# Products with Wu in column tiles of 32, four in turn over two tiles; the halo rows of the automaton network held for two rows of blocks at a time

## The chip, the cores and the metric

The kernel runs on one core of a Trainium2 chip. The metric is device time in microseconds (us), the median of repeated executions. A trace shows one profiled execution: its span runs from the first to the last instruction. The engines named below are TensorE (PE; its weight loads are listed apart as PEld), VectorE (DVE), ScalarE (ACT), GpSimd (POOL) and SyncE (SP), which here only issues DMA transfers.

## The reference: what is computed

The input x is 32 images of 8 channels, 256 x 256, float32. Four layers follow, each `x = x + layer(groupnorm(x))`. Only layer 0 is touched by the change:

```python
drive = x[:, :C_OUT]
grid = drive
for _ in range(15):                       # a coupled-map automaton
    mapped = R * grid * (1.0 - grid)
    local = conv3x3_per_channel(mapped, K_local)
    physics = (1.0 - EPS) * mapped + EPS * local
    grid = (1.0 - BETA) * physics + BETA * drive
cml_out = clip(grid, 0.0001, 1.0 - 0.0001)
h = relu(conv3x3(x, Wp, bp))              # 8 -> 128 channels
nca_out = sigmoid(conv1x1(h, Wu, bu))     # 128 -> 8 channels
gin = concat([x, cml_out, nca_out])       # 24 channels
g = sigmoid(conv1x1(relu(conv3x3(gin, Wg1, bg1)), Wg2, bg2))
layer0 = g * cml_out + (1.0 - g) * nca_out
```

Layers 1 to 3 are 3x3 and 5x5 convolutions of 8 channels. The product with Wu has 128 inputs and only 8 outputs for a pixel.

## The kernel before

There are two phases. The first (lines 148 to 450) computes layer 0 of all images and stores them in DRAM; the second (from line 453) computes layers 1 to 3. The change lies in the first.

An image of 256 rows is seen as 16 blocks (k) of 16 rows (r). Two streams of work are written as generators and interleaved by the loop at line 442.

`lattice(b)` is the automaton for image b. It loads and normalizes the image, transposes it into patches, and makes 15 steps. A step treats the eight channels in two halves of four. For each channel TensorE makes two products, one with the patches themselves (line 278) and one with a ring of neighbours (line 279), both float32 and 512 columns wide; DVE makes two operations on the result (lines 286 and 288); and after each half four DMA transfers on SP copy the new neighbours to `rings` (`spread`, line 210). The next step's ring products of that half wait for these transfers.

`gated(b)` is the rest of layer 0 for the image before, whose data the automaton has finished. It runs over eight values of r2, and each covers two blocks k = 2 r2 and 2 r2 + 1, in all their rows: 16 values of r, 2 x 256 pixels each.

- `hidden(r2)` brings nine-fold shifted input to `im` (6 transfers on ACT's queue for each half of eight rows). For each row r it makes the product with Wp (line 359: 72 inputs, 128 outputs, 512 columns) to a PSUM tile `ph`, applies ReLU on ACT into `hh` (line 364), and multiplies `hh` with Wu (line 343). This product is issued one row late. Its result has 8 useful rows, and it is to land on partitions 8 r to 8 r + 7 of one PSUM tile `psn`; so the stationary matrix is a window of 128 columns in a wide zero matrix `wu_sb`, in which Wu stands at column 8 r, and the 16 products accumulate. Then ACT takes the sigmoid into `nh` (line 370), and two transfers on SP copy the rows which neighbouring row groups need from `nh` to `hb` (`beside`, line 312).
- `gate(r2)` is run after `hidden(r2 + 1)`, since it needs the halo of the blocks below. It makes nine products for the three sources and three column shifts (line 392), one with the halo `ha` of x and the automaton (line 397, called the wga product), one with `hb` (line 398, the wgb product), ReLU, the product with Wg2 (line 403), sigmoid, and the mix on POOL and DVE.

The order of instructions on each engine is made by a scheduler when the program is built: it takes the traced instructions by priority, which follows the order of the text, and lets later ones pass those that it holds not to be ready. [...] The PSUM tiles of `ph`, `pg`, `pq` and the transposes share three buffers; `hh`, `g1` and `gt` share three buffers in SBUF.

Of the kernel before, what the change touches and what calls it, by code (L numbers as in the profile page):

```python
# [9 lines left out]
F32 = mybir.dt.float32  # L10
# [8 lines left out]
C = 8  # L19
# [41 lines left out]
def kernel(  # L61
# [10 lines left out]
    def const(pool, src, shape, name):  # L72
        t = pool.tile(shape, F32, name=name)
        nc.sync.dma_start(t, src)
        return t
# [72 lines left out]
    with ExitStack() as es:  # L148
# [13 lines left out]
        wu_sb = const(wt, wu, [P, 2 * P - C], "wu_sb")  # L162
# [23 lines left out]
        nh = wt.tile([P, HB, WP], F32, name="nh")  # L186
        ha = wt.tile([96, HB, WP], F32, name="ha")
        hb = wt.tile([72, HB, WP], F32, name="hb")
        state = wt.tile([P, C, SN], F32, name="state")
        rings = [wt.tile([RING, 4, SN], F32, name=f"rings{i}") for i in range(2)]  # L190
        for t in (xb, nh, ha, hb, state, *rings):
            nc.gpsimd.memset(t, 0.0)
# [119 lines left out]
        def beside(queue, t, src, q, blocks):  # L312

            k0, n = blocks
            for i, (p, to) in enumerate(((P - C, k0 + 1), (0, k0 - 1))):
                skip, last = max(0, -to), max(0, to + n - HB)
                m = n - skip - last
                row = HB * WP
                long = m * WP - 2
                queue.dma_start(  # L320
                    t[q + 24 * i : q + 24 * i + 24, :, :].rearrange("p k w -> p (k w)")[
                        :, (to + skip) * WP : (to + skip) * WP + long
                    ],
                    window(src, p * row + (k0 + skip) * WP, [[row, C], [1, 3], [1, long]]),
                )

        def gated(b):

            xn, xr, nr, cr = xn_d[b % 2], xr_d[b % 2], nr_d[b % 2], cr_d[b % 2]
            beside(nc.gpsimd, ha, nr, 0, (0, HB))
            beside(nc.gpsimd, ha, cr, 48, (0, HB))
# [4 lines left out]
            def hidden(r2):  # L338
                pn = ps_n.tile([P, 512], F32, name="psn")
                late = None  # L340

                def second(hh, r):
                    nc.tensor.matmul(  # L343
                        pn, wu_sb[:, C * (RB - 1 - r) : C * (RB - 1 - r) + P], hh,
                        start=r == 0, stop=r == RB - 1,
                    )

                for half in range(2):
                    im = imp.tile([72, 2, 8 * WP], F32, name="im")
                    for dy in range(3):  # L350
                        for k in range(2):
                            at = ((2 * r2 + k) * RB + 8 * half + dy) * WP
                            nc.scalar.dma_start(
                                im[24 * dy : 24 * dy + 24, k, 0:run],
                                window(xn, at, [[HP * WP, C], [1, 3], [1, run]]),
                            )
                    for j in range(8):
                        ph = psum.tile([P, 512], F32, name="ph", tag="ps")
                        nc.tensor.matmul(  # L359
                            ph.rearrange("p (k w) -> p k w", w=W), wp_sb,  # L360
                            im[:, :, j * WP : j * WP + W], start=True, stop=True,
                        )
                        hh = hp.tile([P, 512], F32, name="hh")
                        nc.scalar.activation(hh, ph, AF.Relu, bias=bp_sb)  # L364
                        if late is not None:
                            second(*late)
                        late = (hh, 8 * half + j)
                        yield
                second(*late)
                nc.scalar.activation(  # L370
                    nh[:, 2 * r2 : 2 * r2 + 2, 1 : 1 + W],
                    pn.rearrange("p (k w) -> p k w", w=W), AF.Sigmoid, bias=bu_sb,
                )
                beside(nc.sync, hb, nh, 0, (2 * r2, 2))
# [3 lines left out]
            def gate(r2):  # L378
                k0 = 2 * r2
                if r2 % 2 == 0:  # L380
                    for name, t in (("xq", nr), ("cq", cr)):
                        quarter[name] = qp.tile([P, 4, WP], F32, name=name)
                        nc.scalar.dma_start(quarter[name], t[:, k0 : k0 + 4, :])
# [6 lines left out]
                for s, src in enumerate((xq, cq, nh[:, k0 : k0 + 2, :])):  # L390
                    for dx in range(3):
                        nc.tensor.matmul(  # L392
                            o, wg1_sb[:, s, dx, :], src[:, :, dx : dx + W],
                            start=s == dx == 0, stop=False,
                        )
                    yield
                nc.tensor.matmul(o, wga_sb, ha[:, k0 : k0 + 2, 0:W], start=False, stop=False)  # L397
                nc.tensor.matmul(o, wgb_sb, hb[:, k0 : k0 + 2, 0:W], start=False, stop=True)  # L398
                g1 = hp.tile([P, 512], F32, name="g1", tag="hh")
# [4 lines left out]
                gt = hp.tile([P, 2, W], F32, name="gt", tag="hh")  # L404
                nc.scalar.activation(gt.rearrange("p r w -> p (r w)"), pq, AF.Sigmoid, bias=bg2_sb)  # L405
                ci = cq[:, :, 1 : 1 + W]
                ni = nh[:, k0 : k0 + 2, 1 : 1 + W]
# [185 lines left out]
def laid_out(inputs):  # L593
# [68 lines left out]
    wu = np.zeros((P, 2 * P - C), f)  # L662
    wu[:, P - C : P] = inputs["L0_conv_Wu"][:, :, 0, 0].T
# [15 lines left out]
    for g in range(4):  # L679
# [8 lines left out]
        wu=wu,  # L688
# [43 lines left out]
```

## Time and profile before

| | |
|---|---|
| median of 3 runs | 23432.1 us (23431.12 to 23445.79) |
| profiled execution | 23433.82 us, span 23432.0 us |
| mean granted TensorE clock | 0.962 |
| busy share PE, DVE, ACT, POOL | 94%, 35%, 17%, 5% |
| products with Wp (L359), with Wu (L343) | 8192 records each |
| automaton's products (L278, L279) | 7680 records each |
| last store of the automaton (L308), first | 407.6 us; last one 17906.1 us |

In a row of the profile a name such as `psn<-hh,wu_sb` says what the instruction writes and reads, L343 is a line of the kernel, and xN a count; after the bar stand busy time, mean nanoseconds of one, and the engine's idle time just ahead of these instructions with what ended it. A float32 product shows up as two matmul records and two weight loads.

### The profile page before, as it was taken

The page shows a single profiled execution, that of the slowest core. Times are in us where ns is not written, and L with a number is a line of the kernel's source. Part 1 is how long each engine was busy: PE and PEld are TensorE (multiplying, and loading weights), DVE is VectorE, ACT ScalarE, POOL GpSimd, SP SyncE. Part 2 cuts the span into 40 slices and gives each one's busy share as a digit, 9 for nine tenths or more (in the row PEclk, how much of TensorE's full clock was granted, in tenths as well). Part 3 has the DMA queues.
Part 4 walks back from the last instruction along what each step waited for, and adds up shares of the span by engine and source line. Part 5 has one row for each costly group of instructions (what it writes and reads, how often), then busy time and mean ns, then how long its engine had stood idle before and what let it go on. Part 6 is the DMA issues. An engine that isn't in the chain of part 4 may idle for free.

```text
span 23432.0 us, 148223 instructions
## 1 busy us (share of the span) xinstructions
PE 21942.2 (94%) x52808; PEld 9629.6 (41%) x52808; DVE 8279.5 (35%) x13690; ACT 4064.1 (17%) x5794; POOL 1160.9 (5%) x1071
## 2 busy tenths in 40 slices
PE   7999999999999999999999999999999899999999
PEld 3444444444444444444444444444444344444444
DVE  4333333333333333333333333333332223223222
ACT  0222222222212222221212222122122100000000
POOL 0000000000000000000000000000000000000000
PEclk8999999999999999999999999999999999999999
DMA  5444444444444444444444444444443111111111
GB/s 106 110 111 109 110 109 110 110 112 109 110 110 109 109 111 110 113 107 110 115 110 112 112 110 110 110 109 110 110 111 85 60 58 54 53 52 54 54 50 47
DMA packets 623925, 2269.01 MB, mean 97 GB/s; under 512 B 103160, under 2 KB 302472, under 8 KB 461400
## 3 DMA queue, kind: packets, MB, share of 16 engines
q1 hardware_dynamic: 346200, 997.10, 20.9%
q10 hardware_dynamic: 172032, 810.61, 12.1%
q0 software_dynamic: 104960, 451.82, 6.6%
q8 instruction: 424, 6.95, 0.1%
q14 instruction: 309, 2.53, 0.0%
HBM read 1130.77 MB, written 471.37 MB: 68 GB/s over the span
## 4 chain that ended last, share of the span: by engine, by line
PE 87%; DMA 6%; DVE 5%; ACT 1%; issue 1%; POOL 0%; SPq 0%; ACTq 0%; DVEq 0%; POOLq 0%
PE psn L343 15%; PE ph L359 15%; PE psc L279 13%; PE psc L278 13%; PE psv L496 10%; PE psv L570 9%; PE pg L392 7%; DMA xb<-in_x 2%; DMA cr_d<-xb 1%; PE pq L403 1%; DMA im<-xn_d 1%; PE pg L398 1%; PE pg L397 1%; DMA hb<-nh 1%; DVE bn L234 1%
## 5 line engine op out<-in xcount | busy, mean ns | idle before, releaser
L286 DVE SCALAR_TENSOR_TENSOR state<-psc,dr 128x512 f32<-128x512 f32 x3840 | 2625.5, 689 | 7848.0 <-PE psc L279 6693.4
L359 PE MATMUL ph<-im,wp_sb 72*128 72x512 f32 x8192 | 4201.0, 611 | 115.2 <-DMA hb<-nh 56.1
L343 PE MATMUL psn<-hh,wu_sb 128*128 128x512 f32 x8192 | 4228.0, 608 | 28.5 <-ACT hh L364 28.3
L364 ACT ACTIVATE hh<-ph,bp_sb 128x512 f32<-128x512 f32 x4096 | 2809.5, 687 | 8164.5 <-PE ph L359 6633.6
L278 PE MATMUL psc<-state,patch_sb 128*128 128x512 f32 x7680 | 3919.2, 596 | 105.2 <-DVE state L286 103.4
L279 PE MATMUL psc<-rings,ring_sb 80*128 80x512 f32 x7680 | 3916.5, 594 | 32.4 <-DMA rings<-state 32.4
L288 DVE SCALAR_TENSOR_TENSOR state<-state 128x512 f32<-128x512 f32 x3584 | 2461.7, 706 | 64.4
L359 PEld LDWEIGHTS ph<-im,wp_sb 72*128 72x128 f32 x8192 | 1591.0, 195 | 2145.1 <-issue 1432.2
L343 PEld LDWEIGHTS psn<-hh,wu_sb 128*128 128x128 f32 x8192 | 1532.4, 193 | 2174.0 <-issue 1723.4
L278 PEld LDWEIGHTS psc<-state,patch_sb 128*128 128x128 f32 x7680 | 1449.4, 190 | 2007.4 <-issue 1757.8
L279 PEld LDWEIGHTS psc<-rings,ring_sb 80*128 80x128 f32 x7680 | 1459.9, 190 | 1898.6 <-issue 1880.5
L570 PE MATMUL psv<-xr,w_sb 128*128 128x512 f32 x5120 | 2220.8, 592 | 7.3 <-DVE xr L560 7.3
L496 PE MATMUL psv<-xh,w_sb 128*128 128x512 f32 x4608 | 1987.9, 593 | 23.4 <-ACT xh L128 23.4
L570 PEld LDWEIGHTS psv<-xr,w_sb 128*128 128x128 f32 x5120 | 960.7, 189 | 1201.7 <-issue 1197.2
L496 PEld LDWEIGHTS psv<-xh,w_sb 128*128 128x128 f32 x4608 | 868.4, 189 | 1129.6 <-issue 1093.0
L411 POOL TENSOR_TENSOR gt<-gt,df 128x512 f32<-128x512 f32 x256 | 324.5, 1267 | 14360.0 <-ACT gt L405 14360.0
L400 ACT ACTIVATE g<-pg,bg_sb 128x512 f32<-128x512 f32 x256 | 175.9, 687 | 3924.1 <-PE pg L398 3371.6
L542 DVE SCALAR_TENSOR_TENSOR x<-psv,b_sb,x 128x512 f32<-128x512 f32 x256 | 192.2, 751 | 1676.8 <-PE psv L496 1676.8
L576 DVE TENSOR_TENSOR y<-psv,y 128x512 f32<-128x512 f32 x256 | 176.9, 691 | 1564.8 <-PE psv L570 1564.8
L392 PE MATMUL pg<-cq,wg_sb 128*128 128x512 f32 x1536 | 716.6, 592 | 0.0
L392 PE MATMUL pg<-xq,wg_sb 128*128 128x512 f32 x1536 | 701.8, 592 | 0.0
L392 PE MATMUL pg<-nh,wg_sb 128*128 128x512 f32 x1536 | 700.9, 592 | 0.0
(132 smaller groups left out, 8705.6 us busy)
## 6 DMA issues: line engine op xcount, KB each, us to landing
im<-xn_d ACTq DMA_DIRECT2D x3072, 193.3 KB
rings<-state SPq DMA_DIRECT2D x1920, 213.8 KB
rings<-state SPq DMA_DIRECT2D x1920, 142.5 KB
xn_d<-xb POOLq DMA_DIRECT2D x32, 2064.0 KB, 23.8
nr_d<-xb POOLq DMA_DIRECT2D x32, 2064.0 KB, 33.6
xq<-nr_d ACTq DMA_DIRECT2D x128, 516.0 KB
cr_d<-xb POOLq DMA_DIRECT2D x32, 2064.0 KB, 10.2
cq<-cr_d ACTq DMA_DIRECT2D x128, 516.0 KB
```

Source lines behind the costliest of these rows:

```text
L234: nc.vector.bn_stats(bn[:, r, :], xb[:, r, 1 : 1 + W])
L278: nc.tensor.matmul(o, patch_sb[:, c, :], v, start=True, stop=False)
L279: nc.tensor.matmul(o, ring_sb[:, c, :], rings[half][:, c % 4, 0 : TX * SY].rearrange("p (x y) -> p x y", y=SY)[:, :, 0:TY], start=False, s ...
L286: nc.vector.scalar_tensor_tensor(v, o, FLOOR, dr[:, c], ALU.max, ALU.add)
L288: nc.vector.scalar_tensor_tensor(v, v, 1.0, v, ALU.subtract, ALU.mult)
L343: nc.tensor.matmul(pn, wu_sb[:, C * (RB - 1 - r) : C * (RB - 1 - r) + P], hh, start=r == 0, stop=r == RB - 1,)
L359: nc.tensor.matmul(ph.rearrange("p (k w) -> p k w", w=W), wp_sb, im[:, :, j * WP : j * WP + W], start=True, stop=True,)
L364: nc.scalar.activation(hh, ph, AF.Relu, bias=bp_sb)
L392: nc.tensor.matmul(o, wg1_sb[:, s, dx, :], src[:, :, dx : dx + W], start=s == dx == 0, stop=False,)
L411: nc.gpsimd.tensor_tensor(gt, gt, df, ALU.mult)
L496: nc.tensor.matmul(o, w[:, tap, :], src[:, 2 * r + dy : 2 * r + dy + 2, dx : dx + W], start=tap == 0, stop=tap == 8,)
L570: nc.tensor.matmul(o, w3_sb[:, 0 if part == 0 else 1 + k, dx, :], xr[:, k if part == 0 else 1 - k, 2 * g : 2 * g + 2, dx : dx + W], start= ...
```

## The change

Products with Wu go to column tiles. TensorE's array is used as four independent tiles of 32 output columns each; `wu_sb` becomes four matrices of 32 columns, with Wu at column 0, 8, 16 or 24. Row r = 4 q + i goes to column tile q with the matrix i, and lands on partitions 32 q + 8 i. Only four products accumulate on a tile's partitions.

The rows are taken in the order 0, 4, 1, 5, 2, 6, 3, 7 in each half. After four products with Wp, four `hh` tiles stand in the list `late`; their products with Wu are issued together, after the second product of the next four, and their tiles alternate: q, q + 1, q, q + 1. `hh` gets six buffers, `g1` and `gt` get three of their own.

The halo `hb` had all 16 blocks' rows; now there are two tiles of two rows each, filled by `beside_two` at the start of `gate(r2)` and no longer at the end of `hidden(r2)`. So that the transfer needs no cases at the image's edge, `nh` has a row of zeros at each end and its content is shifted by one row.

```diff
-        nh = wt.tile([P, HB, WP], F32, name="nh")
+        nh = wt.tile([P, HB + 2, WP], F32, name="nh")
-        hb = wt.tile([72, HB, WP], F32, name="hb")
+        hbs = [wt.tile([72, 2, WP], F32, name=f"hb{i}") for i in range(2)]
...
+        def beside_two(hb, k0):
+
+            row, long = (HB + 2) * WP, 2 * WP - 2
+            for i, (p, at) in enumerate(((P - C, k0), (0, k0 + 2))):
+                nc.sync.dma_start(
+                    hb[24 * i : 24 * i + 24, :, :].rearrange("p k w -> p (k w)")[:, 0:long],
+                    window(nh, p * row + at * WP, [[row, C], [1, 3], [1, long]]),
+                )
...
-                late = None
-
-                def second(hh, r):
-                    nc.tensor.matmul(
-                        pn, wu_sb[:, C * (RB - 1 - r) : C * (RB - 1 - r) + P], hh,
-                        start=r == 0, stop=r == RB - 1,
-                    )
+                late = []
+
+                def second():
+                    for hh, r in late:
+                        q, i = divmod(r, 4)
+                        nc.tensor.matmul(
+                            pn[32 * q : 32 * q + 32, :], wu_sb[:, i, :], hh,
+                            start=i == 0, stop=i == 3,
+                        )
+                    late.clear()
...
-                    for j in range(8):
-                        ph = psum.tile([P, 512], F32, name="ph", tag="ps")
...
-                        hh = hp.tile([P, 512], F32, name="hh")
-                        nc.scalar.activation(hh, ph, AF.Relu, bias=bp_sb)
-                        if late is not None:
-                            second(*late)
-                        late = (hh, 8 * half + j)
-                        yield
-                second(*late)
+                    for rows in ((0, 4, 1, 5), (2, 6, 3, 7)):
+                        four = []
+                        for i, j in enumerate(rows):
+                            ph = psum.tile([P, 512], F32, name="ph", tag="ps")
...
+                            hh = hp.tile([P, 512], F32, name="hh", bufs=6)
+                            nc.scalar.activation(hh, ph, AF.Relu, bias=bp_sb)
+                            four.append((hh, 8 * half + j))
+                            if i == 1:
+                                second()
+                            yield
+                        late += four
+                second()
...
-                beside(nc.sync, hb, nh, 0, (2 * r2, 2))
...
             def gate(r2):
                 k0 = 2 * r2
+                hb = hbs[r2 % 2]
+                beside_two(hb, k0)
...
-                nc.tensor.matmul(o, wgb_sb, hb[:, k0 : k0 + 2, 0:W], start=False, stop=True)
-                g1 = hp.tile([P, 512], F32, name="g1", tag="hh")
+                nc.tensor.matmul(o, wgb_sb, hb[:, :, 0:W], start=False, stop=True)
+                g1 = hp.tile([P, 512], F32, name="g1", tag="gt", bufs=3)
```

## The prediction

> **What bounds the kernel now.** I read the page first: busy shares, the chain of work that ended last, the costliest groups.
>
> ```profile
> PE 21942.2 (94%) x52808; PEld 9629.6 (41%) x52808; DVE 8279.5 (35%) x13690; ACT 4064.1 (17%) x5794; POOL 1160.9 (5%) x1071
> ...
> PE 87%; DMA 6%; DVE 5%; ACT 1%; issue 1%; POOL 0%; SPq 0%; ACTq 0%; DVEq 0%; POOLq 0%
> PE psn L343 15%; PE ph L359 15%; PE psc L279 13%; PE psc L278 13%; PE psv L496 10%; PE psv L570 9%; PE pg L392 7%; DMA xb<-in_x 2%; DMA cr_d<-xb 1%; PE pq L403 1%; DMA im<-xn_d 1%; PE pg L398 1%; PE pg L397 1%; DMA hb<-nh 1%; DVE bn L234 1%
> ...
> L343 PE MATMUL psn<-hh,wu_sb 128*128 128x512 f32 x8192 | 4228.0, 608 | 28.5 <-ACT hh L364 28.3
> ...
> L279 PE MATMUL psc<-rings,ring_sb 80*128 80x512 f32 x7680 | 3916.5, 594 | 32.4 <-DMA rings<-state 32.4
> ```
>
> TensorE sets the time: 87% of the chain, and the products with Wu (L343), the ones that change, are its largest line at 15%. Its waits are tiny: 28.5 us in front of L343, 32.4 us in front of the ring products. Each float32 product leaves two records (8192 for 4096).
>
> Second, the stretches: automaton alone (first image), steady state, a boundary between images, the last image's gates alone.
>
> ```profile
> 100.00:400.00 300.00, 249.41 (x467) 97.58 (x465) 148.21 (x235) 0.00 (x0) 0.56 (x2) 0.86 0.48 77
> 500.00:900.00 400.00, 398.33 (x919) 172.26 (x918) 159.37 (x235) 74.20 (x108) 20.50 (x17) 1.00 0.46 99
> 1520.00:1560.00 40.00, 15.18 (x49) 7.86 (x48) 15.55 (x44) 4.23 (x6) 9.60 (x11) 0.71 0.74 218
> ...
> 17950.00:18300.00 350.00, 315.12 (x645) 132.13 (x643) 27.57 (x35) 96.51 (x139) 26.57 (x23) 0.90 0.22 64
> ```
>
> Columns: stretch, then busy time of PE, PEld, DVE, ACT, POOL; then TensorE clock, DMA share, GB/s. In steady state PE is busy 398 of 400 us at full clock. Where the automaton stands alone, PE waits and the clock falls to 0.86. The boundary idles some 25 us an image and isn't touched.
>
> Third, the timeline of PE, in two places: prices of a product, and the automaton alone.
>
> ```profile
> 8020.67 1.02 PE L279 MATMUL psc<-rings,ring_sb 80*128 80x512 f32 x2
> 8021.67 1.12 PE L403 MATMUL pq<-g,wg_sb 128*128 128x512 f32 x2
> 8022.63 1.88 PE L359 MATMUL ph<-im,wp_sb 72*128 72x512 f32 x4
> ```
>
> ```profile
> 204.69 2.74 PE L279 MATMUL psc<-rings,ring_sb 80*128 80x512 f32 x6
> ...
> 210.85 1.92 PE L279 MATMUL psc<-rings,ring_sb 80*128 80x512 f32 x2
> 212.56 2.81 PE L278 MATMUL psc<-state,patch_sb 128*128 128x512 f32 x6
> 215.20 2.74 PE L279 MATMUL psc<-rings,ring_sb 80*128 80x512 f32 x6
> ...
> 225.51 1.02 PE L279 MATMUL psc<-rings,ring_sb 80*128 80x512 f32 x2
> ```
>
> A record takes 0.43 us of the pipe (x6 lasts 2.74, x2 lasts 1.02: 1.72/4), a product 0.86; the extra 0.16 of a row is the modelled tail of the last record. L403 had waited, so its weights were loaded in the open: its successor starts 0.96 later, not 0.86; an open load of 128 columns costs 0.10. The second fence shows the automaton's own loop: the last ring product of one half starts at 210.85, the first of the same half in the next step at 225.51. Those 14.66 us (DVE's two operations, four transfers on SP) are what the loop needs when nothing else is in the way.
>
> **What the Trainium skill says.** "TensorEngine Tiling (Array Packing)", Tiling Modes, Key Properties: tiles work independently, but changing the mode, not just the tile, drains TensorE. The trace has no such change amid other products, so it shows neither. "TensorE: Matmul & The Clock Gate", Part 3: three column tiles measured 2.38x; matmuls start and end in program order. It doesn't say whether for float32, and no run here shows it. Same page, LDWEIGHTS: time is columns / 1.2 GHz, so 107 ns for 128 and 27 for 32; the 0.10 above agrees. Same page, Part 1: an idle window of about 3.4 us halves the clock; the 0.86 and 0.71 above agree in kind.
>
> **The change, part by part.**
>
> *Overlap.* The Wu product has 32 output columns instead of 128 but still streams 512 columns twice in each of two records; a product alone costs 0.86 as before. The gain is in overlap. With order A, B, A, B and two records each (A1 A2 B1 B2 ...), A2 can't overlap A1 (same tile), B1 overlaps A2, the next A1 overlaps B2: a run of n alternating products takes n+1 slots of 0.43 instead of 2n. The built order of the changed program does not keep the fours together: of 1651 runs on PE 521 have four products, 280 three, 322 two, 528 one, because a block's last products wait for their ReLU and are put between gate products. Slots: 521x5 + 280x4 + 322x3 + 528x2 = 5747 against 8192. Gain 2445 x 0.43 = 1051 us.
>
> *Mode changes.* Each run is entered and left: 3302 changes, none before. Bounds for the pair: below, only the array's depth, about 0.06 each way (estimate from that page's 128-cycle drain at 2.4 GHz) plus open loads 0.03 and 0.10: 0.25 us. Above, the whole tail of 0.16 and the full duration of a load record (0.19 for 128 columns, L343's PEld row; 0.08 for the small load of the column-tile product at L135): 0.59. I take 0.16 + 0.03 + 0.16 + 0.10 = 0.45, as a drain reads as waiting out the tail: 1651 x 0.45 = 743 us (413 to 974).
>
> *The automaton's wait.* What follows on PE is moved too. Between the last ring product of a half and the first of that half in the next step, PE's queue holds at least 18.1 us of work before (steady images, 0.86 a product). In the changed order three of an image's 28 such places hold 10.3, 10.3 and 11.2 us, all automaton work, between the product with wga and the one with wgb: the automaton has run ahead and the rest of the gate waits for the halo. It needs 14.66, so PE waits 4.4 + 4.4 + 3.5 = 12.3 us an image, times 31 overlapped images 381 us. Below: 0, if the transfers are quicker there. Above: each wait of over 3.4 us also costs clock; half speed for 3.4 us afterwards is 1.7 us lost, x3 x31 = 158. I take half of that, 80. PE is first in first out: behind a waiting ring product stand the wgb product, the gate's last product and the next block's im products.
>
> *Halo of nh for one block (hb).* Before, 512 transfers on SP (448 of 48.2 KB, 64 of 24.0 KB), each pair after its block's sigmoid; after, 512 of 48.2 KB, each pair when the next block's sigmoid is done, the same moment on which the lower row depended anyway. SP's order past the ring transfers hardly moves. The sigmoid comes up to three gate products (2.6 us) later, as the last two Wu products are put among them; 8.2 us of PE work still lie between the last Wu product and wgb at the least (8.6 before), and that cover held L398's own wait to 10.7 us in all. I take 0; without cover, 1 us for each of 256 blocks would be 256.
>
> *The rest costs nothing:* six hh buffers and separate g1/gt ones only loosen ACT (busy 17%); products with Wp keep number and size; nh with two more rows and the smaller hb change memsets at the start by a few us under weight loads.
>
> Sum on the profiled execution (23433.8; span 23432.0, median of the runs 23432.1, so no shift): -1051 + 743 + 381 + 80 = +153, so 23590 us.
>
> **Rivals.** *Cheap changes, faster.* All as above, but a pair of mode changes costs 0.25: 413. -1051 + 413 + 381 + 80 = -177: 23255; without the ring waits 22800. It decides from a pair below (1051 - 461)/1651 = 0.36 us. For it: loads are prefetched two ns after the product ahead starts, so TensorE is good at hiding; against: the drain forbids just that.
>
> *No overlap.* Float32 products in two column tiles run one after the other: the 1051 falls away, 23434 + 743 + 461 = 24640; with cheap changes 24310. For it: nothing shown proves overlap in float32; against: the skill's measured 2.38x.
>
> *The change finds no slack to use:* overlap works, but the automaton's loop (10.4 us a half-step alone: 204.69, 215.20, 225.51) becomes the bound. Against: 30 half-steps at 10.4 are 312 us of an image period of 564 (cr_d's first and last stores, 407.6 and 17906.1, over 31). Only locally, as priced; its time is the forecast's.
>
> **How the numbers follow.** Forecast, overlap eaten by changes and waits: 0.44, own range 23385 to 23950. Cheap changes: 0.28, all faster than 23385. No overlap: 0.28, 24200 to 24700. Within 0.2% (47 us), which is about what a measurement of this kernel can tell from no change, lies 0.09 of the forecast's 0.44. Faster 0.28, same 0.09, slower 0.63. The range leaves 0.1 at each end: 23020 to 24600.
>
> **What would show it.** Right: records of the Wu products starting in pairs almost together, a run of four filling about 2.15 us; about 0.2 us of extra idle where a run begins and ends; waits of ring products for their transfers of some 12 us an image instead of 1; DVE, ACT and the second phase (after 18.3 ms) unchanged. Wrong: starts at an even 0.43 (no overlap); no extra idle at a run's ends; the clock below 1.00 in steady state throughout, which I haven't priced; waits for hb ahead of the wgb product.

## The result, and the profile after

The changed kernel takes 24053.2 us (median of 4 runs, 24041.23 to 24109.03), against 23431.6 us before on the same chip (4 runs, 23419.65 to 23445.79). The ratio is 1.027, 95% interval 1.0252 to 1.0288: 622 us slower. The forecast was 153 us slower. The sign held, the size did not: the time lies above the range given to the forecast itself (23385 to 23950 us), and inside the outer one (23020 to 24600). The profiled execution has a span of 24039.4 us and a mean TensorE clock of 0.926, down from 0.962.

The page of the changed kernel, with the lines that answer to those shown before (L351 is the product with Wu, L370 the product with Wp):

```profile
PE 21730.1 (90%) x52808; PEld 8619.8 (36%) x52808; DVE 8083.0 (34%) x13690; ACT 4075.7 (17%) x5794; POOL 1148.0 (5%) x1072
...
PE 78%; DMA 11%; DVE 7%; issue 1%; ACT 1%; POOL 1%; SPq 1%; DVEq 0%; ACTq 0%; POOLq 0%
...
L370 PE MATMUL ph<-im,wp_sb 72*128 72x512 f32 x8192 | 4312.0, 659 | 448.7 <-DMA im<-xn_d 261.8
L278 PE MATMUL psc<-state,patch_sb 128*128 128x512 f32 x7680 | 3920.1, 624 | 584.1 <-DVE state L286 581.6
L351 PE MATMUL psn<-hh,wu_sb 128*32 128x512 f32 x8192 | 2538.8, 628 | 0.0
```

The products with Wu now keep TensorE busy for 2538.8 us instead of 4228.0, with as many records. Yet all of TensorE's busy time falls by only 212 us, and its share of the chain falls from 87% to 78%: DMA and DVE have taken 11% and 7%. Idle time stands in front of two lines, L370 and L278, that had little: 448.7 and 584.1 us, against 115.2 and 105.2 before.

A run of Wu products in the timeline of PE (start, length, line, tile, count of records):

```profile
560.59 1.02 PE L370 MATMUL ph<-im,wp_sb 72*128 72x512 f32 x2
561.54 1.91 PE L351 MATMUL psn<-hh,wu_sb 128*32 128x512 f32 x8
563.38 2.84 PE L370 MATMUL ph<-im,wp_sb 72*128 72x512 f32 x6
```

The eight records of four products take 1.84 us from their first start to their successor's. Without a change of mode, L351 would have started 0.86 after L370, at 561.45; it started at 561.54. So the whole run costs 1.93 us, where four products cost 3.44 before. Single records, taken over all such runs by the median, start 0.521 us after the record ahead (0.43 is normal), then in pairs: 0.007, 0.447, 0.007, 0.423, 0.007, 0.423, 0.007, and the successor 0.523 after the last. Two column tiles work at the same time and fully so, and each change of mode costs 0.09 us.

The stretches, columns as before (TensorE's clock is the number after the five busy times):

```profile
500.00:900.00 400.00, 378.66 (x914) 145.07 (x913) 147.18 (x229) 72.19 (x105) 17.25 (x15) 0.98 0.45 99
8110.00:8560.00 450.00, 431.43 (x1024) 165.09 (x1023) 165.85 (x258) 81.59 (x119) 21.87 (x19) 0.96 0.43 97
8204.21:8228.10 23.89, 23.12 (x28) 8.12 (x30) 7.81 (x12) 5.50 (x8) 3.45 (x3) 0.50 0.19 59
```

The second line is the steady part of a middle image. The third line is a part of it: for 23.9 us TensorE is busy and runs at half clock. In the steady part of the image that I compared, the kernel before has a clock of 1.00 (8430 to 8780 us).

PE's waits, first of the kernel after, then of the kernel before (total, times, longest):

```profile
PE psc L278 <- DVE state L286: 581.6, 293, 8.9
...
PE ph L370 <- DMA im<-xn_d: 261.8, 25, 14.8
...
PE ph L370 <- DMA rings<-state: 168.6, 13, 15.0
PE psc L279 <- DMA rings<-state: 128.0, 54, 25.1
```

```profile
PE psc L278 <- DVE state L286: 103.4, 90, 8.7
...
PE ph L359 <- DMA hb<-nh: 56.1, 17, 6.6
PE ph L359 <- DMA im<-xn_d: 51.0, 15, 5.9
PE psc L279 <- DMA rings<-state: 32.4, 10, 25.4
```

Two kinds of wait grew. The waits of the automaton's products (the two psc rows; called the loop's waits below) went from 135.8 to 709.6 us. The first of these rows names DVE, and what DVE itself had waited for divides it: 460.8 of the 581.6 us stand behind an operation L286 that waited for ring transfers, and 115.0 behind the gate's mix, which has its place ahead of L286 in DVE's list (51.3 and 51.3 us before). The wait of the Wp product for its input went from some 113 to some 443 us; a wait for several semaphores is put down to the last of them, so rows of ph that name rings or hb are counted in (168.6 and, not shown, 13.0 after; 56.1 and, not shown, 6.3 before).

**The first wait, in the middle of an image.** Timeline of PE, with the idle time in brackets:

```profile
8197.71 2.74 PE L278 MATMUL psc<-state,patch_sb 128*128 128x512 f32 x6
8201.76 1.13 PE L279 MATMUL psc<-rings,ring_sb 80*128 80x512 f32 x2 [1.31 <-DMA rings<-state]
8204.98 2.07 PE L411 MATMUL pg<-hb,wgb_sb 72*128 72x512 f32 x2 [2.10 <-DMA hb<-nh]
8206.85 3.62 PE L279 MATMUL psc<-rings,ring_sb 80*128 80x512 f32 x4
```

The ring product waits, L411 (with wgb) behind it waits as well, and at 8204.21 the clock halves: from there two records last 2.07 us instead of 1.02, for the 23.9 us shown above. This is one of the long cases: in the 31 overlapped images the half clock at this place lasts 10.2 us in 18 and over 20 us in six. The forecast had not named this place. Its three places, automaton work between the product with wga and the one with wgb, come later in the image, at 8282.6, 8422.3 and 8498.0. The second of them, in the same view, with DVE and SP at that time:

```profile
8415.68 2.74 PE L279 MATMUL psc<-rings,ring_sb 80*128 80x512 f32 x6
8422.25 1.70 PE L278 MATMUL psc<-state,patch_sb 128*128 128x512 f32 x2 [3.83 <-DVE state L286]
...
8429.20 1.02 PE L411 MATMUL pg<-hb,wgb_sb 72*128 72x512 f32 x2
```

```profile
8415.26 6.00 SPq L218 DMA_DIRECT2D rings<-state  x4
8421.50 1.29 DVE L286 SCALAR_TENSOR_TENSOR state<-psc,dr 128x512 f32<-128x512 f32 x2 [6.31 <-DMA rings<-state]
```

No ring product waits here: the three at 8415.68 follow without a gap. What waits is L286 on DVE, for ring transfers issued from 8415.26 on. They carry the half just finished, while L286 writes the channels of the other half, into the same tile `state` from which the transfers read. Until L286 has emptied one of the three PSUM buffers of `psc`, the fourth product of its half, L278 at 8422.25, can't start. Whether the wait of L286 for the other half's transfers is needed, no run here tests.

From the normal start of the successor (records 0.43 apart) the three waits are 3.3, 4.0 and 4.8 us, 12.1 together, with 3.4, 3.4 and 6.8 us of half clock. Five more, of about 1 us each, lie in the same image, four of them behind the gate's mix on DVE.

**The second wait, at the start of an image,** once for each. Timelines of DVE, ACT and PE:

```profile
8062.31 2.50 DVE L265 SCALAR_TENSOR_TENSOR state<-dr 128x512 f32<-128x512 f32 x4 [9.81 <-DMA rings<-state]
```

```profile
8055.84 0.69 ACT L382 ACTIVATE nh<-psn,bu_sb 128x512 f32<-128x512 f32 x1 [2.79 <-PE psn L351]
8055.84 3.88 ACTq L362 DMA_DIRECT2D im<-xn_d  x2
8064.91 3.62 ACT L270 ACTIVATE dr<-dr 128x4096 f32<-128x4096 f32 x1 [8.38 <-DMA im<-xn_d]
8064.93 0.66 ACTq L362 DMA_DIRECT2D im<-xn_d  x1
```

```profile
8054.71 1.05 PE L351 MATMUL psn<-hh,wu_sb 128*32 128x512 f32 x4
8067.95 4.61 PE L370 MATMUL ph<-im,wp_sb 72*128 72x512 f32 x5 [12.19 <-DMA rings<-state]
```

Read from the end: the Wp product at 8067.95 had waited 12.2 us for `im`. The last transfer of that input was issued on ACT's queue at 8064.93, just behind L270 (8064.91), which stands ahead of it in ACT's list. L270 scales the automaton's drive and needs what DVE has made of it at L265. DVE's last four operations there began at 8062.31, after 9.8 us in front of the first ring transfers of the new image. So the input of one stream stood behind a chain of the other one. Two transfers ahead of it were issued only at 8055.84, when the sigmoid L382 started, which needs the last Wu product. The clock halves at 8060.85, again for 23.9 us, 16.8 of which are busy.

**The sum.** Medians of the runs of Wu products, mode changes included: 521 runs of four at 1.932 us, 280 of three at 1.926, 322 of two at 1.073, 528 of one at 1.067, together 2455 us, against 4096 x 0.86 = 3523. TensorE gained 1068 us. The kernel lost 622, so 1690 us were lost elsewhere. The waits above account for 574 + 330 us, less 109 for a wait of the group norm at the boundary of images that became shorter: 795. Half clock while TensorE was busy cost 30.1 us an image instead of 7.0, over the 31 periods between the first and the last store of the automaton: 23.1 x 31 = 716. Of the remaining 179 us a new wait of the transposes (L299 for DVE's copy L302) is 54.4; the rest these views don't place.

### The profile page after: what moved, and what is told of

It is laid out like the page before. It is cut to its first block, busy times and chain, and to the rows that moved or that the text cites. A ratio compares the mean times of both kernels' runs of the same rounds, so it can differ in the third digit from the quotient of the medians.

```text
span 24039.4 us, 145434 instructions
## 1 busy us (share of the span) xinstructions
PE 21730.1 (90%) x52808; PEld 8619.8 (36%) x52808; DVE 8083.0 (34%) x13690; ACT 4075.7 (17%) x5794; POOL 1148.0 (5%) x1072
## 3 DMA queue, kind: packets, MB, share of 16 engines
q10 hardware_dynamic: 172032, 810.61, 12.2%
## 4 chain that ended last, share of the span: by engine, by line
PE 78%; DMA 11%; DVE 7%; issue 1%; ACT 1%; POOL 1%; SPq 1%; DVEq 0%; ACTq 0%; POOLq 0%
PE ph L370 14%; PE psc L278 13%; PE psc L279 12%; PE psv L509 10%; PE psn L351 9%; PE psv L583 9%; PE pg L405 8%; DMA rings<-state 7%; DMA xb<-in_x 2%; DMA im<-xn_d 1%; PE pq L416 1%; DVE state L286 1%; PE pg L411 1%; POOL gt L424 1%; DVE xc L426 1%
## 5 line engine op out<-in xcount | busy, mean ns | idle before, releaser
L286 DVE SCALAR_TENSOR_TENSOR state<-psc,dr 128x512 f32<-128x512 f32 x3840 | 2569.5, 687 | 7976.4 <-PE psc L279 4536.1
L370 PE MATMUL ph<-im,wp_sb 72*128 72x512 f32 x8192 | 4312.0, 659 | 448.7 <-DMA im<-xn_d 261.8
L278 PE MATMUL psc<-state,patch_sb 128*128 128x512 f32 x7680 | 3920.1, 624 | 584.1 <-DVE state L286 581.6
L279 PE MATMUL psc<-rings,ring_sb 80*128 80x512 f32 x7680 | 3958.2, 621 | 129.2 <-DMA rings<-state 128.0
L370 PEld LDWEIGHTS ph<-im,wp_sb 72*128 72x128 f32 x8192 | 1636.4, 208 | 2900.5 <-issue 2666.1
L351 PE MATMUL psn<-hh,wu_sb 128*32 128x512 f32 x8192 | 2538.8, 628 | 0.0
L278 PEld LDWEIGHTS psc<-state,patch_sb 128*128 128x128 f32 x7680 | 1469.5, 198 | 2749.6 <-issue 1664.0
L288 DVE SCALAR_TENSOR_TENSOR state<-state 128x512 f32<-128x512 f32 x3584 | 2344.5, 686 | 28.5
L279 PEld LDWEIGHTS psc<-rings,ring_sb 80*128 80x128 f32 x7680 | 1509.3, 198 | 2149.9 <-issue 2022.6
L351 PEld LDWEIGHTS psn<-hh,wu_sb 128*32 128x32 f32 x8192 | 431.2, 111 | 1837.6 <-issue 1835.4
L425 DVE TENSOR_TENSOR gt<-gt,nh 128x512 f32<-128x512 f32 x256 | 177.5, 693 | 2552.8 <-POOL gt L424 2552.8
L405 PE MATMUL pg<-xq,wg_sb 128*128 128x512 f32 x1536 | 789.5, 623 | 0.0
```

The lines of the kernel that those rows point to most:

```text
L278: nc.tensor.matmul(o, patch_sb[:, c, :], v, start=True, stop=False)
L279: nc.tensor.matmul(o, ring_sb[:, c, :], rings[half][:, c % 4, 0 : TX * SY].rearrange("p (x y) -> p x y", y=SY)[:, :, 0:TY], start=False, s ...
L286: nc.vector.scalar_tensor_tensor(v, o, FLOOR, dr[:, c], ALU.max, ALU.add)
L288: nc.vector.scalar_tensor_tensor(v, v, 1.0, v, ALU.subtract, ALU.mult)
L351: nc.tensor.matmul(pn[32 * q : 32 * q + 32, :], wu_sb[:, i, :], hh, start=i == 0, stop=i == 3,)
L370: nc.tensor.matmul(ph.rearrange("p (k w) -> p k w", w=W), wp_sb, im[:, :, j * WP : j * WP + W], start=True, stop=True,)
```

## The experiments

My theory after the result: the column tiles gain, and waits with the half clock behind them eat the gain. The rivals: the column tiles themselves lower the clock or cost more than they save; the halo by two blocks is late; the order by fours, with its six buffers, makes the waits, whatever the width of the products. In the counts below and above, a record of TensorE is counted without its last 0.15 us, the tail that is drawn over the next record; "idle" is the time without a record, and "half clock" the busy time lost to it, both for one image period; some 8 us of the idle time of kernels with column tiles are their mode changes (3302 gaps of 0.08 us between records).

### The halves of the change

The second half alone: the kernel after with the products, their order and their buffers as before.

```diff
# against after
-                        nc.tensor.matmul(
-                            pn[32 * q : 32 * q + 32, :], wu_sb[:, i, :], hh,
-                            start=i == 0, stop=i == 3,
-                        )
...
+                    nc.tensor.matmul(
+                        pn, wu_sb[:, C * (RB - 1 - r) : C * (RB - 1 - r) + P], hh,
+                        start=r == 0, stop=r == RB - 1,
+                    )
...
-                    for rows in ((0, 4, 1, 5), (2, 6, 3, 7)):
...
+                    for j in range(8):
```

> The kernel before with the second half of the change alone (halo of nh in two tiles of two rows, filled at the start of the gate; products with Wu as before). If the halo is neutral, as predicted: 23350 to 23550 us, waits of PE as before. If the moved halo transfers are what costs (rival): over 23800, with waits for hb ahead of the wgb product.

Measured: 23345.4 us, ratio to before 0.9962 (0.9948 to 0.9976). A late halo is not the cause: the new halo is, if anything, a small gain. From this kernel to after, the first half of the change costs 708 us.

The same kernel as after but with products of 128 columns, so order by fours, buffers and halo stay:

```diff
# against after
-                        q, i = divmod(r, 4)
                         nc.tensor.matmul(
-                            pn[32 * q : 32 * q + 32, :], wu_sb[:, i, :], hh,
-                            start=i == 0, stop=i == 3,
+                            pn, wu_sb[:, C * (RB - 1 - r) : C * (RB - 1 - r) + P], hh,
+                            start=r == 0, stop=r == RB - 1,
```

> The changed kernel with its products with Wu in the new order and in fours, but 128 columns wide, so without column tiles. If the new waits come from TensorE being done sooner (theory): TensorE has its old work back, so 23350 to 23600 us and few ring waits. If the order by fours, the late ReLU products or the buffers cost by themselves (rival): 23900 or more.

Measured: 23387.9 us, 0.9978 (0.997 to 0.9987). The loop's wait (L278 for DVE) is 74.5 us in all. The text's order by fours makes no waits by itself. From this kernel to after, only the column tiles are added, and they cost 665 us.

### Without the automaton's exchange

Both leave out the ring exchange inside the steps, so the automaton computes with rings that are never renewed.

```diff
-                    if step < STEPS - 1:
-                        spread(half)
```

> The kernel before without the ring transfers after each half-step (it leaves out the exchange of the automaton's neighbours after the first; the first one stays). Both theories: the kernel before hardly waits for them, so 23100 to 23430 us.

> The changed kernel with the same left out. If waits for the automaton's loop, and the half clock after them, eat the gain (theory): 1068 us of TensorE time come to light, less what the wait for im at an image's start keeps: 22400 to 23000 us, clock 1.00 inside an image. If column tiles themselves lower the clock or slow their neighbours (rival): over 23500, clock below 0.98 inside an image.

Measured (one run each): before without exchange 23201.1 us, after without exchange 22752.9 us. With nothing to wait for in the automaton's loop, the change is a gain of 448 us. Two stretches of the second kernel, each most of an image:

```profile
5850.00:6280.00 430.00, 430.00 (x1062) 166.91 (x1062) 183.51 (x270) 85.78 (x125) 20.14 (x19) 1.00 0.20 58
6400.00:6850.00 450.00, 447.47 (x1118) 175.89 (x1117) 190.82 (x280) 87.15 (x127) 24.74 (x23) 1.00 0.21 62
```

Full clock with column tiles throughout: the tiles don't lower it. What stands between 448 and 1068 is above all the wait at the start of an image, which needs no ring exchange between the steps: 13.8 us at 6382, with 23.9 us of half clock. The idle time is 48.6 us an image against 34.5 in the first of the two kernels, and half clock costs 16.4 us against 7.1.

### The wait at the start of an image

The second stage's input is not loaded; it takes that of the first. This leaves out 12 of an image's 96 transfers to `im`.

```diff
-                    im = imp.tile([72, 2, 8 * WP], F32, name="im")
-                    for dy in range(3):
+                    if r2 != 1:
+                        ims[half] = imp.tile([72, 2, 8 * WP], F32, name="im")
+                    im = ims[half]
+                    for dy in range(3 if r2 != 1 else 0):
```

> The changed kernel in which the second of an image's eight hidden stages takes the input tiles of the first again (it leaves out 12 of 96 im transfers of an image and computes that stage on the first's input). If the wait for im at an image's start, 12 us and then 24 us at half clock, is a loss of its own (theory): 24 us less for each of 31 images, about 23300 us, and no long wait before the second stage. If it is only a place where a loss shows that would come elsewhere (rival): 23900 or more.

Measured (one run): 23536.5 us, 517 less than after. The wait for `im` is gone; the loop's wait rose from 581.6 to 866.0 us. So the wait at an image's start is real, but part of it comes back as ring waits.

Is `im` late because of the store of `nr_d`, which shares the DMA engines with it? That store moved to the automaton's fourth step:

```diff
-            nc.gpsimd.dma_start(on_rows(nr_d[b % 2], WP), xb)
...
+                if step == 3:
+                    nc.gpsimd.dma_start(on_rows(nr_d[b % 2], WP), xb)
```

> The changed kernel with the store of the normalized image (nr_d, 2064 KB) moved from the image's start to the automaton's fourth step; the order on TensorE stays as it is. If im comes late because it shares the DMA engines with this store: the wait of 12 us shrinks below 5, and 23300 to 23700 us. If im is late since its buffers come free late or ACT issues it late: no change, 24000 to 24100 us.

Measured: 24051.4 us, 1.026 (1.0243 to 1.0277): no different from after. The store is not the cause.

Issue the transfers of `im` in the text right behind the half that frees their buffer, one stage early:

```diff
+            ims = [load(0, 0), load(0, 1)]
...
-                    im = imp.tile([72, 2, 8 * WP], F32, name="im")
...
+                    im = ims.pop(0)
...
+                    if r2 + 1 < NCH:
+                        ims.append(load(r2 + 1, half))
```

> The changed kernel with the im transfers of the next stage's half traced, and so issued on ACT's queue, right after the half that frees the buffer, ahead of the sigmoid and of the automaton's long ACT operation; all work is done. In TensorE's order no place has less than 15.7 us between a half's last and next first ring product. If im is late because its issue stands behind those in ACT's queue, and the ring waits come from the order that follows from it (theory): both losses go, 22350 to 22800 us. If the transfers are simply too slow for the faster TensorE (rival): 23500 or more, with waits for im spread over all stages.

Measured: 23476.5 us (20 runs, 23383.4 to 23562.2, the slowest of them traced), 1.0017 (1.0007 to 1.0027): 577 less than after, but above the range expected. The wait for `im` is out of the list of long waits, and another stands at the same place, in PE's waits:

```profile
PE psc L279 <- DMA rings<-state: 379.0, 84, 26.0
```

In the middle image the ring product waits 9.7 us at the start of the automaton (8467.6), with 20.5 us of half clock. The hole was moved, not closed.

The control, with products, row order and buffers as before, and new halo and early transfers:

> The kernel before with the new halo and the same early im transfers, products with Wu 128 wide: TensorE is the bound there already and has hardly a wait to lose, so 23250 to 23400 us. The difference to the run with the changed kernel is then what column tiles are worth once nothing else holds: 550 to 1000 us.

Measured: 24651.9 us, 1.0519 (1.0503 to 1.0534), a clear miss: with the wide products, early transfers do harm. In its list of waits, Wu products waiting for their ReLU rose to 304.3 us. By this measure the first half of the change is a gain of 1175 us (24651.9 to 23476.5), which says as much of the control's poor order as of the column tiles.

### The ring waits in the middle of an image

The gate one stage later, its halo as early as in after, so that the products with wga and wgb stand elsewhere:

```diff
-            for r2 in range(NCH + 1):
+            for r2 in range(NCH + 2):
...
-                if r2 > 0:
-                    yield from gate(r2 - 1)
+                if 0 < r2 <= NCH:
+                    beside_two(hbs[(r2 - 1) % 2], 2 * (r2 - 1))
+                if r2 > 1:
+                    yield from gate(r2 - 2)
```

> The changed kernel with each gate run one stage later (after the next hidden stage but one), its halo transfers issued where they were. Then the wgb product waits for nothing and the automaton isn't run ahead while it waits; in TensorE's order at least 16.5 us of work lie between a half's last and next first ring product instead of 10.3. If the automaton's loop waits come from that order (theory): about 1000 us less than the changed kernel, 22950 to 23250 us, with only the wait for im left. If they come from the transfers themselves being too slow for the faster TensorE (rival): 23800 or more.

Measured: 23553.1 us, 1.0051 (1.0036 to 1.0066). The loop's wait fell from 581.6 to 91.4 us, the wait for `im` stayed (236.9 and 177.6), and Wp products wait 182.6 us for ReLUs that weren't there before. Half of the expected gain came. With the late store of `nr_d` as well:

> Both of the last two edits together. If the two losses are separate and both edits cure theirs: 22300 to 22750 us, below the kernel before and the changed kernel, clock at 1.00 inside an image. If im is late for another reason than the store: as the run with the gate later alone.

Measured: 23544.3 us, 1.0045 (1.003 to 1.006): the same. And with the early transfers of `im`:

> The changed kernel with early im transfers and the gate one stage later. Theory: little left for the second edit, within 150 us of the run with early im alone. If the halo's wait ahead of the wgb product still costs there: 200 us or more below it.

Measured: 23997.5 us, 1.0234 (1.0219 to 1.0249), a miss: two edits that gain 500 and 577 us alone give 56 together. The loop's waits are back: 553.1 us for DVE, and 345.9 for the rings, against 128.0 in after.

A PSUM buffer of their own for `pg` and `pq`, so that the gate no longer shares three buffers with `ph` (`psn` gives up its second one):

```diff
-        ps_n = es.enter_context(tc.tile_pool(name="ps_n", bufs=2, space=PSUM))
+        ps_n = es.enter_context(tc.tile_pool(name="ps_n", bufs=1, space=PSUM))
...
-                pg = psum.tile([P, 512], F32, name="pg", tag="ps")
+                pg = psum.tile([P, 512], F32, name="pg", tag="pg", bufs=1)
...
-                pq = psum.tile([P, 512], F32, name="pq", tag="ps")
+                pq = psum.tile([P, 512], F32, name="pq", tag="pg", bufs=1)
```

First together with the early transfers of `im`:

> The changed kernel with early im transfers and a PSUM buffer of their own for the gate's two results (ps_n has one buffer instead of two), so that products with Wp can pass a waiting gate. Theory: within 150 us of the run with early im alone; a gain above that says that the gate still held up the products behind it.

Measured: 23173.6 us, 0.9883 (0.9866 to 0.9899): the fastest kernel that does all the work, faster than the kernel before and than after, and 303 us below the run with the early transfers alone, where up to 150 were expected: by that measure the gate had still held up the products behind it. Idle time is still 57.5 us an image, and half clock costs 23.3. Then alone:

> The changed kernel with a PSUM buffer of their own for the gate's two results (ps_n one buffer instead of two), im transfers as in the changed kernel. One place an image is left with less than 14.66 us of TensorE work between a half's last and next first ring product, against three. If the ring waits come from products with Wp that can't pass a waiting gate (theory): most of the ring waits go and the wait for im stays, 23100 to 23500 us. If the loop is too slow in any order (rival): 23850 or more.

Measured: 23603.6 us, 1.0066 (1.0051 to 1.0081), just above the range. In PE's waits:

```profile
PE pg L405 <- DMA cq<-cr_d: 343.2, 31, 14.9
...
PE psc L278 <- DVE state L286: 173.5, 125, 9.8
```

The wait of L278 for DVE is down by 408 us, the wait for `im` stays (223.5, 193.9 and 102.0 us under three names), and a wait of 11 us for the gate's own input appears at each boundary between images. The control, with products, row order and buffers as before, the new halo, and the PSUM buffer:

> Control: the kernel before with the new halo and the same PSUM buffers; TensorE hardly waits there. Theory: within 100 us of the run with the new halo alone (23345 us).

Measured: 23275.9 us, 0.9929 (0.9912 to 0.9945). So the new buffer helps the old products by 69 us, and beside it the first half of the change costs 328 us. And the PSUM buffer together with the second stage's input left out, as above:

> The changed kernel with the gate's own PSUM buffers and, in addition, the second hidden stage of an image on the input tiles of the first (it leaves out 12 of 96 im transfers of an image). Theory: both waits mostly gone, 22500 to 23000 us, which is the 1068 us of TensorE time less what is left of ring waits. If another wait takes their place (rival): over 23200.

Measured (one run): 23169.9 us, above the range: the wait for `cq` stays at 341.5 us.

### Is it the order or the speed?

TensorE could wait for the rings because it reaches the ring product sooner, or because the list of instructions has less work in front of it, whatever that work takes. Rows in natural order send all four products of a group to one tile in turn:

```diff
-                    for rows in ((0, 4, 1, 5), (2, 6, 3, 7)):
+                    for rows in ((0, 1, 2, 3), (4, 5, 6, 7)):
```

> The changed kernel with rows in the order 0 to 7, so that the four products of a group go to one column tile after another row of it, not in turn over two tiles. If the gain is overlap between tiles: records of a run start 0.42 to 0.43 us apart each, a run of four takes about 3.6 us, and TensorE being no faster than before, its waits shrink; 23600 to 24200 us. If a product in a column tile is cheaper in itself: starts closer than 0.42 us.

Measured (one run): 25099.3 us, above the range. Timeline of PE, and its waits:

```profile
8007.80 1.02 PE L370 MATMUL ph<-im,wp_sb 72*128 72x512 f32 x2
8008.75 3.62 PE L351 MATMUL psn<-hh,wu_sb 128*32 128x512 f32 x8
8012.31 1.13 PE L370 MATMUL ph<-im,wp_sb 72*128 72x512 f32 x2
```

```profile
PE psc L278 <- DVE state L286: 561.3, 342, 8.9
```

In one tile there is no overlap: from 8008.66 (8007.80 + 0.86) to 8012.31 are 3.65 us for four products, with records 0.429 us apart; a product of 32 columns is no cheaper than one of 128. TensorE's work is 525 us an image, more than before (520), so it doesn't come sooner. Yet L278 waits for DVE about as long as in after (561.3 against 581.6 us; at least 304.4 of them behind ring transfers, 180.4 behind the gate's mix). The built list shows why: between a half's last ring product and its first in the next step there are again places with only 10.3 us of PE's work, short by 13.0 us an image (12.2 in after), and in the kernel with wide products by fours there are none (18.9 at least). So these waits don't need a faster TensorE; they go with the list, and the list differs where products of 32 columns stand in the text in place of 128 (wide products in this row order were not run). That the scheduler takes these for cheaper, and so puts less between the ring products, is the likely reason, but I have only seen its lists.

Such a count can be set against the waits of other kernels too. Over 31 images, these are the time by which the places are short, and what the automaton's products waited after an image's first step: wide by fours 0 and 28 us, gate later 0 and 0, own PSUM buffer 28 and 78, after 377 and 585, one tile in turn 404 and 526. The count fails for two kernels with early transfers: gate later (48 and 501) and own PSUM buffer (1 and 275).

## Why the forecast was right in sign and wrong in size

| term | forecast | measured |
|---|---|---|
| overlap of the Wu products | -1051 | -1372 (1068 + 304) |
| mode changes | +743 | +304 |
| ring waits, 31 images (measured: all waits of the automaton's products) | +381 | +574 |
| half clock | +80 | +716 |
| wait for `im` at an image's start | not in the sum | +330 |
| halo | 0 | about 0 (alone: 86 us faster) |
| other (boundary -109, remainder +179) | 0 | +70 |
| sum | +153 | +622 |

*Overlap* was under-sized. The step "a run of n takes n + 1 slots" let neighbours of one tile exclude each other in program order, A1 A2 B1 B2; the records instead start in pairs 7 ns apart, so a run of four takes four slots, and one of three the same four. Which record runs with which can't be seen, but the gain is overlap of two tiles, as the kernel with one tile shows. The step rested on the Trainium skill, "TensorE: Matmul & The Clock Gate", Part 3, that matmuls start in order; and "TensorEngine Tiling (Array Packing)", Key Properties, says that tiles can work in parallel, which this trace confirms for float32.

*Mode changes* were over-sized. I took 0.45 us a pair because a drain "reads as waiting out the tail"; measured are 0.521 - 0.430 = 0.091 and 0.523 - 0.430 = 0.093, so 0.184 a pair, and 1651 x 0.184 = 304. That lies under my lower bound of 0.25: the tail drawn in a record is not time that the next mode waits for. The rival *cheap changes* came nearest to the price (0.25) and had the wrong end: it put the kernel at 23255. TensorE's own gain was even larger than its 638 us, and was lost in waits and half clock, which this rival priced as the forecast did. *No overlap* is refuted.

*The automaton's wait* had its places right and a step of its mechanism wrong. The three places found in the built order wait, 12.1 us in the middle image where 12.3 was forecast. But there no ring product waits for its transfers: the patch product L278 waits for L286, and L286 for the transfers of the other half. The 14.66 us that the loop "needs" were also read too high: the last ring product of that fence runs at half clock (two records in 1.92 us instead of 1.02), which leaves some 13.8 at full clock, and the quickest passage in after takes 13.6. So part of the nearness of 12.1 to 12.3 is luck. The term was too small, 574 against 381, because the automaton's products also wait at places that the order did not show as short, 1.5 us at 8201.8 among them, and 64 us more behind the gate's mix on DVE (115.0 against 51.3).

*The clock* is the step that failed most. "Half speed for 3.4 us afterwards" at half weight gave 80 us; measured are 716. About 220 of them stand at the three places that the forecast priced; the rest stands where it priced no half clock: about 170 at the place of 8201.8, 160 more than before at the wait for `im`, 115 more at the boundary between images. Waits of 1.5 and 2.3 us with one product between them were followed by 23.9 us of half clock, others of 3.3 to 4.8 us by 3.4 or 6.8. The Trainium skill, "TensorE: Matmul & The Clock Gate", Part 1, has a busy window of about 3.4 us restoring the clock; here TensorE was busy for 23.1 of 23.9 us at half clock, and the measurement decides.

*The wait for `im`* was not in the sum. I counted ring products in the built order and not ACT's list, in which transfers of `im` stand behind operations of the other stream. Together with its half clock it is what is left when the ring exchange is gone, where 448 of 1068 us showed. The third rival, *no slack to use*, came nearest in kind: the work saved on TensorE was given back as waits. But I let it end at the forecast's own time, so it added nothing. Its argument, 312 us of loop in a period of 564, is a mean, and the waits come where the list is thin.

The rest held: hb ahead of the wgb product waits 11.8 us in all (10.7 before), and from the last store of the automaton to the end it is 5543 us (5526 before).

Still open: the 1068 us were never had with all the work done. Not run is the kernel with `state` in two tiles, one for each half, which would tell whether L286 has to wait for the other half's transfers at all; nor is the first half of the change with the old halo. The best kernel, with an own PSUM buffer and early transfers, is 102 us faster than the best one without column tiles that ran here. Whether another order closes the hole at the boundary between images, which moved from `im` to the rings to `cq` in turn, these runs don't say. Nor do they say why half clock lasts 3.4 us in one place and 23.9 in another.

## What to carry to other kernels

A cheaper product on the engine that sets the time is worth only what the instruction lists let through: where transfers of a second stream are hidden behind that engine's work, count the work between each need and its transfer in the built order, on every queue that issues a transfer, before counting the gain. Follow a wait to its end: the row named DVE, and DVE stood behind transfers. Price a wait on TensorE with the half clock behind it, which here cost about as much as the waits themselves. And test each part both with and without its neighbours: here the same column tiles, or the half of the change that holds them, measured from 1175 us gained to 708 lost, by what stood beside them.

## What the runs showed of the hardware

- Float32 products of 512 columns in two column tiles overlap fully: records start 7 ns apart in pairs, and four products take 1.75 us without the mode changes, against 3.44 with 128 columns. In one tile they don't overlap: 0.429 us from record to record.
- A change between 128 columns and column tiles costs 0.09 us each way.
- Half clock can last 23.9 us, 23.1 of them busy, after waits of 1.5 and 2.3 us with one product between them; after waits of 3.3 to 4.8 us it lasted 3.4 or 6.8 us.
